# Image statistics dealt differently to half rounds, gather addresses cast in pairs, offset products issued behind the out-projection

## The chip, the cores and the metric

The kernel runs on one core of one Trainium2 chip. The metric is the device time of one execution in microseconds (us), the median of several runs. A profiled execution gives the trace from which every reading below is taken; it is one execution, with a time of its own.

## The reference

Eight images `x` of 512 channels and 64 x 64 pixels pass two layers, each of the form x = x + f(group_norm(x)).

```
x = x + deform_attention(_gn(x), w_q, w_off1, b_off1, w_off2, w_kv, w_out, b_out)
x = x + bottleneck(_gn(x), conv_w, ..., out_b)

# deform_attention, per image:
q     = w_q @ x                                   # 512 x 4096 pixels, 8 groups of 64 channels
t     = gelu(q[:, ::4, ::4] * w_off1 + b_off1)    # 16 x 16 sample places in each group
off   = tanh(w_off2 @ t) * 4                      # two offsets for each place and group
feats = bilinear sample of q at (grid + off)      # four neighbours each, weighted
k, v  = w_kv @ feats                              # 256 keys and values
out   = softmax((q * 0.125) . k) v                # 8 heads
y     = w_out @ out + b_out
```

The bottleneck is a 1x1 convolution to 32 channels, a strided depthwise convolution, two fully connected layers, a depthwise transposed convolution, and a 1x1 convolution back to 512 channels. `_gn` takes the mean and variance of groups of 16 channels over a whole image.

## The kernel before, in words

**Images and rounds.** An image is cut in 8 tiles of 512 pixels, a tile's attention in 4 head pairs. A *round* is one head pair of one tile; an image has 32 rounds, r = 0 to 31. In the main loop (the loop over `g` in the big function) a round issues, in this order: `weighted_values` (tile `pa`, L597), every second round `sum_exps` (`pn`, L624), `add_exps` on VectorE (`es`, L609), once in four rounds `invert` (the reciprocal L637 on VectorE and four small DMAs of SyncE), `logits` of the next round (`ps`, L579, with the exponential L587 on ScalarE), a `fill` of work beside it, `project_out` of the head pair of six rounds ago (`pp`, L666, taken out on VectorE by L673 and its statistics by L676), and a second `fill`. The list that a round leaves on TensorE is the same for all images, so the length of a round can be compared between images. Engines work their queues in order; the order of the code is the order of the queues.

**Half rounds.** The two fills make a round two half rounds. `phase[0]` is 0 in the first, ahead of the out-projection, and 1 in the second, behind it. `fill(200)` draws from the generator `next_image(b)` until that yields `None` (or 200 units are used): so a `yield None` ends a half round and a `yield 0` does not. `next_image` counts its half rounds in `slot`: slot 0 is the second half of round 5, odd slots are first halves, and slot 2(r-5) is the second half of round r. Out-projections, and with them the first fill, begin with round 6.

**What the fills carry.** Slots 0 to 26 work on the bottleneck of the image before (`layer1`, ending with `project_beside`, whose products are `po`, L892, in second halves from slot 12) and on the next image: its 8 tiles are loaded from slot 5, and from slot 12 the 32 `bn_stats` of `norm_x` (L201, VectorE) are drawn, 5 or 6 in each second half. A 33rd draw finds the generator at its end, and from the slot after that the four steps of `norm_q` and `group_stats` are drawn, one in each slot: `bn_aggr` (L169) in the first, then the small product `gps` (L173), then `gpsb` (L182), then the normalising of two tiles.

**The next image's queries.** In round 20 of images 1 to 6 `make_q` issues the whole query projection of the next image in one block (`pq`, L275; transposes `pqt`, L324; rows written to the DRAM tile `qd`). The last four transposes go to PSUM tiles that VectorE empties (L332). Behind it come two `tensor_reduce` of VectorE (L286). From then on `samples` holds that image's sampling generator.

**Sampling.** `sample` starts with the offset products (eight 128 x 128 by 128 x 4 products `po`, L424, each of two matmuls) and the tanh (L433, ScalarE), then `yield None`; then 17 short VectorE operations make the positions, weights and row numbers (L435 to L472), and L474 casts all 32 columns of row numbers to int32 (`row`). Then come 20 gather slots. In the first 16 GpSimd issues two gathers each (L518; four gathers fill one tile `g` of 128 x 4 x 2 x 64 numbers, of which there are two buffers); odd ones also hold `weigh` (L484 to L489, VectorE) of the tile whose last gather was issued a round before, and two of them `to_channels` (L494). Where `to_channels` ends, `project_k` and `project_v` follow in rounds 30 and 31.

**The start.** Image 0's sampling is interleaved with image 1's query projection by a loop that gives the projection 6 units of room for a `None` of `sample` and 2 for a 0. Image 1's sampling is begun there by one `next`, and goes on in image 0's rounds from the second half of round 5.

Of the kernel before, what the change touches and what calls it, by code (L numbers as in the profile page):

```python
# [25 lines left out]
HEADS = 8  # L26
# [23 lines left out]
def kernel(  # L50
# [15 lines left out]
    nc = tc.nc  # L66
# [29 lines left out]
    def spot(b, k):  # L96
        j = region[b]
        k %= NT + 1
        return spares[j] if k == 0 else regions[j][:, :, (k - 1) * TP : k * TP]
# [34 lines left out]
    def load_wq():  # L134
        nc.sync.dma_start(wbuf, w_qT.rearrange("(cc p) o -> p cc o", p=P))
# [13 lines left out]
    def col(k, n=1):  # L149
        return vec[:, k : k + n]  # L150
# [10 lines left out]
    def new_stats(which, b):  # L161
        return small.tile([P, NCC, NT, 6], F32, tag=f"st{which}", name=f"st{which}_{b}")
# [35 lines left out]
    def norm_x(b, st, order=range(NT)):  # L198
        for t in order:
            for cc in range(NCC):  # L200
                nc.vector.bn_stats(st[:, cc, t, :], x_tile(b, t)[:, cc, :])  # L201
                yield None
# [207 lines left out]
    def free_of(b):  # L410

        return spot(b, NT)

    def feats_of(b):
        return free_of(b)[:, 2:4, :].rearrange("p a (c k) -> p a c k", c=2)

    def sample(b, qd):

        free, feats = free_of(b), feats_of(b)
        po = ps_mm.tile([P, TP], F32, tag="mm", name=f"po_{b}")  # L420
        for h in range(2):
            for hp in range(NCC):
                k = h * 16 + hp * 4
                nc.tensor.matmul(  # L424
                    po[:, k : k + 4],
                    offset_in[b][h][:, hp * P : (hp + 1) * P],
                    col(V_OFF2, 4),
                    start=True,
                    stop=True,
                )  # L430

        pos = small.tile([P, 32], F32, tag="pos", name=f"pos_{b}")
        nc.scalar.activation(pos, po[:, :32], AF.Tanh)  # L433
        yield None
        nc.vector.scalar_tensor_tensor(  # L435
            pos, pos, OFF_SCALE, cst[:, K_BASE : K_BASE + 32], ALU.mult, ALU.add
        )
        nc.vector.tensor_scalar(pos, pos, 2.0 / 15.0, -1.0, ALU.mult, ALU.add)
        nc.vector.tensor_scalar(pos, pos, 1.0, float(HW), ALU.add, ALU.mult)
        nc.vector.tensor_scalar(pos, pos, -1.0, 0.5, ALU.add, ALU.mult)  # L440


        ci = small.tile([P, 32], I32, tag="ci", name=f"ci_{b}")
        nc.vector.tensor_copy(ci, pos)
        lo = small.tile([P, 32], F32, tag="lo", name=f"lo_{b}")
        wgt = small.tile([P, 2, 32], F32, tag="wgt", name=f"wgt_{b}")
        nc.vector.tensor_copy(lo, ci)
        nc.vector.tensor_tensor(wgt[:, 0, :], lo, pos, ALU.is_gt)
        nc.vector.tensor_sub(lo, lo, wgt[:, 0, :])
        yield 0  # L450
        nc.vector.tensor_scalar(lo, lo, 0.0, float(HW - 2), ALU.max, ALU.min)

        nc.vector.tensor_sub(wgt[:, 0, :], pos, lo)
        nc.vector.tensor_scalar_add(wgt[:, 1, :], wgt[:, 0, :], -1.0)
        nc.vector.scalar_tensor_tensor(wgt, wgt, -1.0, wgt, ALU.mult, ALU.max)
        nc.vector.tensor_scalar(wgt, wgt, -1.0, 1.0, ALU.mult, ALU.add)
        nc.vector.tensor_scalar_max(wgt, wgt, 0.0)
        yield 0
        lov = lo.rearrange("p (hg a) -> p hg a", a=2)
        wgtv = wgt.rearrange("p k (hg a) -> p k hg a", a=2)  # L460
        rowf = small.tile([P, 2, 16], F32, tag="rowf", name=f"rowf_{b}")
        wt = small.tile([P, 2, 16, 2], F32, tag="wt", name=f"wt_{b}")
        nc.vector.scalar_tensor_tensor(
            rowf[:, 0, :], cst[:, K_GRPNO : K_GRPNO + 16], float(N), lov[:, :, 0], ALU.mult, ALU.add
        )
        nc.vector.scalar_tensor_tensor(
            rowf[:, 0, :], lov[:, :, 1], float(HW), rowf[:, 0, :], ALU.mult, ALU.add
        )
        nc.vector.tensor_scalar_add(rowf[:, 1, :], rowf[:, 0, :], float(HW))
        for ky in range(2):  # L470
            for kx in range(2):
                nc.vector.tensor_mul(wt[:, ky, :, kx], wgtv[:, ky, :, 1], wgtv[:, kx, :, 0])  # L472
        row = small.tile([P, 2, 16], I32, tag="row", name=f"row_{b}")
        nc.vector.tensor_copy(row, rowf)  # L474

        held = []
        acc = [free[:, h, :].rearrange("p (g d) -> p g d", d=DH) for h in range(2)]

        def weigh(h, half, ky, g):

            i = h * HEADS + 4 * half
            w = wt[:, ky, i : i + 4, :].unsqueeze(3).to_broadcast([P, 4, 2, DH])
            a = acc[h][:, 4 * half : 4 * half + 4, :]
            nc.vector.tensor_mul(g, g, w)  # L484
            if ky == 0:
                nc.vector.tensor_add(a, g[:, :, 0, :], g[:, :, 1, :])
            else:
                nc.vector.tensor_add(a, a, g[:, :, 0, :])
                nc.vector.tensor_add(a, a, g[:, :, 1, :])  # L489

        def to_channels(h):
            pt = ps_mm.tile([P, TP], F32, tag="mm", name=f"pf_{b}_{h}")
            for cc in range(NCC):
                nc.tensor.transpose(  # L494
                    pt[:, cc * P : (cc + 1) * P],
                    acc[h][:, 2 * cc : 2 * cc + 2, :].rearrange("p g d -> p (g d)"),
                    ident,
                )
            nc.scalar.copy(
                feats[:, :, :, h * P : (h + 1) * P],  # L500
                pt.rearrange("p (a c k) -> p a c k", a=2, c=2),
            )

        steps = [(h, half, ky) for h in range(2) for half in range(2) for ky in range(2)]

        for slot in range(2 * len(steps) + 4):
            n, odd = divmod(slot, 2)
            if odd and n >= 5 and n % 4 == 1:
                to_channels(n // 4 - 1)
            if odd and 1 <= n <= len(steps):  # L510
                weigh(*steps[n - 1], held.pop(0))
            if n < len(steps):
                h, half, ky = steps[n]
                if not odd:
                    held.append(gp.tile([P, 4, 2, DH], F32, tag="g", name=f"g_{b}_{n}"))
                for i in (2 * odd, 2 * odd + 1):
                    k = h * HEADS + 4 * half + i
                    nc.gpsimd.indirect_dma_start(  # L518
                        held[-1][:, i, :, :].rearrange("p j d -> p (j d)"),
                        None,  # L520
                        qd[:, :],
                        bass.IndirectOffsetOnAxis(ap=row[:, ky, k : k + 1], axis=0),
                    )
            yield None
# [467 lines left out]
    phase = [1]  # L992
# [4 lines left out]
    def next_image(b):  # L997

        n = b + 1
        if b:  # L1000
            free = spot(b - 1, 0)
            first = layer1(b - 1, st1s.pop(b - 1), project_beside, free, free[:, 0:2, :])
            other, blocks = iter(()), ()
            if n < B:
                st = new_stats(0, n)
                blocks = norm_x(n, st)
                other = norm_q(n, st, norms)


            first_load = 5  # L1010
            ahead = 4
            slot = 0
            while first:
                if blocks is None and ahead:
                    next(other)
                    ahead -= 1
                if next(first, "end") == "end":
                    first = None
                if n < B:
                    if first_load <= slot < first_load + NT:  # L1020
                        load_x(n, (slot - first_load,), nc.gpsimd)
                    if slot == first_load + 2 * NT:
                        load_wq()
                    if phase[0] and slot > first_load + 6:
                        for _ in range(6 if slot in (first_load + 13, first_load + 15, first_load + 17) else 5):
                            if blocks and next(blocks, "end") == "end":
                                blocks = None
                slot += 1
                yield None
            if n < B:  # L1030
                drain(other)
                while n not in samples:
                    yield None
        if n < B:
            yield from samples[n]
# [6 lines left out]
    samples = {}  # L1042
# [15 lines left out]
    with tc.manual_schedule():  # L1058
# [38 lines left out]
        for g in range(len(names) + LAG):  # L1097
# [44 lines left out]
            k = g + 1 - LAG  # L1142
# [132 lines left out]
```

## Time and profile before

| | |
|---|---|
| runs (3) | 3301.49 us median, 3300.69 to 3302.63 |
| the profiled execution | 3300.22 us, of which the program's span 3298.4 us |
| TensorE matmul | 3212.1 us busy, 97% of the span |
| VectorE | 2321.9 us busy, 70% |
| ScalarE | 1187.9 us busy, 36% |
| GpSimd | 606.2 us busy, 18% |
| granted TensorE clock, mean | 0.99 |

A line of the timeline has a start and a duration in us, the engine, the line of the code, the operation, the tile it writes and those it reads, and, in brackets, how long the engine had been idle and what released it. In the view of waits a line names who waited, for whom, how long in total, how often, and the longest. A window's line gives busy time and count of each engine, the granted clock, and the DMA's share and GB/s. PE is TensorE, PEld its weight loads, DVE VectorE, ACT ScalarE, POOL GpSimd, SP SyncE.

### The profile page before, as it was taken

Reading aid. Unit: us, or ns where it says so; the run is one execution under the profiler, and the core shown is the slowest. Engines: PE = TensorE matmul, PEld = TensorE weight load, DVE = VectorE, ACT = ScalarE, POOL = GpSimd, SP = SyncE. Lnnn points to the kernel's source line nnn. Section 1 sums busy time; section 2 is a strip of 40 time slices with the busy share of each in tenths; the row PEclk is TensorE's granted clock in tenths of the full one; section 3 lists DMA queues with packets and bytes.
Section 4 is the critical chain, followed back from the end, with each engine's and each line's share of the span. In section 5 each row is a group of like instructions: output and inputs, shape, how many; then the busy total and the mean of one; then the engine's idle time right before and its main releaser. Section 6 shows DMA issues by size and latency. Waiting matters only on the chain.

```text
span 3298.4 us, 46059 instructions
## 1 busy us (share of the span) xinstructions
PE 3212.1 (97%) x18196; PEld 1532.3 (46%) x18196; DVE 2321.9 (70%) x3666; ACT 1187.9 (36%) x1641; POOL 606.2 (18%) x576
## 2 busy tenths in 40 slices
PE   6999999999999999999999999999999999999996
PEld 5884223258332583326732276332853338433222
DVE  7885765786757767587766876668766687756565
ACT  2343333344324433344333443335433344333420
POOL 1130300230402204022130312204021040310201
PEclk9999999999999999999999999999999999999996
DMA  7232222662327532284323833257232482322713
GB/s 275 77 99 73 81 69 87 202 134 78 116 77 224 122 90 91 96 224 113 111 85 132 197 91 105 79 188 171 71 97 89 179 179 65 122 71 71 135 38 131
DMA packets 293873, 390.61 MB, mean 118 GB/s; under 512 B 18320, under 2 KB 157840, under 8 KB 293648
## 3 DMA queue, kind: packets, MB, share of 16 engines
q1 hardware_dynamic: 240368, 261.72, 24.3%
q0 software_dynamic: 53280, 125.86, 17.3%
q8 instruction: 145, 2.38, 0.3%
q14 instruction: 80, 0.66, 0.1%
HBM read 193.52 MB, written 192.94 MB: 117 GB/s over the span
## 4 chain that ended last, share of the span: by engine, by line
PE 90%; DVE 6%; issue 2%; DMA 1%; SPq 0%; ACT 0%; POOL 0%; ACTq 0%; DVEq 0%; POOLq 0%
PE pp L666 25%; PE pq L275 24%; PE ps L579 13%; PE pa L597 12%; PE pqt L324 4%; PE pn L624 3%; PE py L749 2%; PE pk L532 2%; PE pv L559 2%; DVE rn L637 1%; PE po L892 1%; DVE st L201 1%; DMA rn<-rn 1%; DVE es L609 1%; DVE rb L650 1%
## 5 line engine op out<-in xcount | busy, mean ns | idle before, releaser
L666 PE MATMUL pp<-image,wout 128*64 128x512 f32 x3584 | 823.5, 602 | 4.9 <-DVE image L652 3.2
L587 ACT ACTIVATE es<-ps 128x1024 f32<-128x1024 f32 x512 | 505.3, 1023 | 289.3 <-PE ps L579 201.3
L666 PEld LDWEIGHTS pp<-image,wout 128*64 128x64 f32 x3584 | 238.0, 137 | 551.8 <-issue 465.5
L597 PE MATMUL pa<-es,vt 128*64 128x512 f32 x2048 | 488.3, 597 | 1.7 <-ACT es L587 1.7
L275 PE MATMUL pq<-image,wbuf 128*128 128x256 f32 x2048 | 476.2, 381 | 1.9 <-DVE image L217 1.9
L518 POOL DMA_INDIRECT g<-qd,row x256 | 274.2, 1071 | 1024.5 <-DVE row L474 842.1
L673 DVE SCALAR_TENSOR_TENSOR image<-pp,vec,image 128x512 f32<-128x512 f32 x224 | 166.8, 745 | 415.4 <-PE pp L666 383.1
L579 PE MATMUL ps<-image,kt 64*64 64x512 f32 x3584 | 442.6, 602 | 1.0
L275 PEld LDWEIGHTS pq<-image,wbuf 128*128 128x128 f32 x2048 | 381.8, 191 | 54.4 <-issue 5.0
L604 ACT COPY image<-pa 128x512 f32<-128x512 f32 x224 | 132.1, 590 | 683.7 <-PE pa L597 628.3
L609 DVE TENSOR_TENSOR es<-es,es 128x1024 f32<-128x1024 f32 x256 | 310.6, 1213 | 71.5 <-PE pa L597 71.4
L597 PEld LDWEIGHTS pa<-es,vt 128*64 128x64 f32 x2048 | 137.3, 136 | 298.0 <-issue 273.9
L579 PEld LDWEIGHTS ps<-image,kt 64*64 64x64 f32 x3584 | 115.5, 132 | 312.1 <-issue 184.6
L637 DVE RECIPROCAL rn<-pn 128x512 f32<-128x512 f32 x64 | 214.7, 3355 | 13.7 <-PE pn L624 6.9
L334 ACT COPY qr<-pqt 128x512 f32<-128x512 f32 x224 | 131.2, 586 | 237.2 <-PE pqt L324 222.2
L185 POOL TENSOR_TENSOR gs<-ve,nhalf 128x4 f32<-128x4 f32 x16 | 16.7, 1042 | 1063.3 <-DVE ve L184 1063.3
L650 DVE STREAM_SHUFFLE rb<-rn 128x512 f32<-128x512 f32 x256 | 187.4, 732 | 0.5 <-issue 0.4
L275 PE MATMUL pq<-es,es 128*128 128x256 f32 x768 | 181.5, 379 | 0.0
L944 POOL DMA_DIRECT2D out_dram<-part x126 | 138.0, 1324 | 161.0 <-ACT part L939 153.7
L201 DVE BATCH_NORM_STATS2 st<-image 128x6 f32<-128x512 f32 x256 | 158.6, 678 | 7.5 <-DMA image<-in_x_dram 7.4
L676 DVE BATCH_NORM_STATS2 st<-image 128x6 f32<-128x512 f32 x224 | 155.6, 695 | 7.7
L652 DVE TENSOR_TENSOR image<-image,rb 128x512 f32<-128x512 f32 x224 | 155.2, 693 | 7.8
(197 smaller groups left out, 3470.2 us busy)
## 6 DMA issues: line engine op xcount, KB each, us to landing
qd<-qr SPq DMA_DIRECT2D x256, 256.0 KB
image<-in_x_dram SPq DMA_DIRECT2D x112, 512.0 KB
out_dram<-image SPq DMA_DIRECT2D x49, 1024.0 KB
image<-in_x_dram POOLq DMA_DIRECT2D x48, 1024.0 KB
out_dram<-part POOLq DMA_DIRECT2D x126, 256.0 KB
image<-in_x_dram SPq DMA_DIRECT2D x16, 1024.0 KB
wbuf<-in_w_kvT_dram SPq DMA_DIRECT2D x14, 1024.0 KB
out_dram<-spare POOLq DMA_DIRECT2D x56, 256.0 KB
```

The lines of the kernel that those rows point to most:

```text
L201: nc.vector.bn_stats(st[:, cc, t, :], x_tile(b, t)[:, cc, :])
L275: nc.tensor.matmul(bank[:, o * 2 * P : (o + 1) * 2 * P], w[:, k, o * P : (o + 1) * P], xh[:, k, :], start=(k == 0), stop=(k == 1),)
L518: nc.gpsimd.indirect_dma_start(held[-1][:, i, :, :].rearrange("p j d -> p (j d)"), None, qd[:, :], bass.IndirectOffsetOnAxis(ap=row[:, ky, ...
L579: nc.tensor.matmul(ps[k : k + DH, a, :], kt[r : r + DH, hp, kc * P + k : kc * P + k + DH], qt[r : r + DH, hp, :], start=True, stop=True,)
L587: nc.scalar.activation(e, ps, AF.Exp)
L597: nc.tensor.matmul(pa[a * DH : (a + 1) * DH, :], vt[:, kc, hd * DH : (hd + 1) * DH], es[kc][:, a, :], start=(kc == 0), stop=(kc == 1),)
L609: nc.vector.tensor_add(es[0], es[0], es[1])
L637: nc.vector.reciprocal(rn, denominators.pop((b, t)))
L650: nc.vector.stream_shuffle(rb, rn, [2 * (hp % 2) + hp // 2] * 32)
L666: nc.tensor.matmul(pp[r : r + DH, :], wout[:, hp, oc * P + r : oc * P + r + DH], ao[:, hp, :], start=(hp == 0), stop=(hp == NCC - 1),)
L673: nc.vector.scalar_tensor_tensor(xt[:, oc, :], pp, col(V_BOUT + oc), xt[:, oc, :], ALU.add, ALU.add)
L676: nc.vector.bn_stats(st[:, oc, t, :], xt[:, oc, :])
```

## The change

Four edits. The tanh of `sample` is followed by `yield 0`, and `next_image` keeps waiting while `phase[0]` is 0: the offset products and the tanh are issued in the second half of round 20, behind the out-projection, in the half round that also holds the positions and the first two gathers. The single cast of all row numbers is replaced by a cast of two columns in each of the first 16 gather slots, ahead of its two gathers. And the statistics are drawn 5 in each second half, and 4 in slot 19, which is the first half of round 15.

```
@@ sample @@
         nc.scalar.activation(pos, po[:, :32], AF.Tanh)
-        yield None
+        yield 0
...
         row = small.tile([P, 2, 16], I32, tag="row", name=f"row_{b}")
-        nc.vector.tensor_copy(row, rowf)
...
                 if not odd:
                     held.append(gp.tile([P, 4, 2, DH], F32, tag="g", name=f"g_{b}_{n}"))
+                k = h * HEADS + 4 * half + 2 * odd
+                nc.vector.tensor_copy(row[:, ky, k : k + 2], rowf[:, ky, k : k + 2])
                 for i in (2 * odd, 2 * odd + 1):
@@ next_image @@
-                    if phase[0] and slot > first_load + 6:
-                        for _ in range(6 if slot in (first_load + 13, first_load + 15, first_load + 17) else 5):
+                    if slot == first_load + 14 or phase[0] and slot > first_load + 6:
+                        for _ in range(5 if phase[0] else 4):
                             if blocks and next(blocks, "end") == "end":
                                 blocks = None
...
                 drain(other)
-                while n not in samples:
+                while n not in samples or phase[0] == 0:
                     yield None
```

`first_load` is 5. Counted from the code, the 32 statistics go to the slots so:

| slot | 12 | 14 | 16 | 18 | 19 | 20 | 22 |
|---|---|---|---|---|---|---|---|
| before | 5 | 5 | 5 | 6 | 0 | 6 | 5 |
| after | 5 | 5 | 5 | 5 | 4 | 5 | 3 |

More of the change, by code (lines that the diff above doesn't have):

```diff
@@ L433, in sample @@
         nc.scalar.activation(pos, po[:, :32], AF.Tanh)
-        yield None
+        yield 0
         nc.vector.scalar_tensor_tensor(
@@ L473, in sample @@
         row = small.tile([P, 2, 16], I32, tag="row", name=f"row_{b}")
-        nc.vector.tensor_copy(row, rowf)
         held = []
@@ L515, in sample @@
                     held.append(gp.tile([P, 4, 2, DH], F32, tag="g", name=f"g_{b}_{n}"))
+                k = h * HEADS + 4 * half + 2 * odd
+                nc.vector.tensor_copy(row[:, ky, k : k + 2], rowf[:, ky, k : k + 2])
                 for i in (2 * odd, 2 * odd + 1):
@@ L1023, in next_image @@
                         load_wq()
-                    if phase[0] and slot > first_load + 6:
-                        for _ in range(6 if slot in (first_load + 13, first_load + 15, first_load + 17) else 5):
+                    if slot == first_load + 14 or phase[0] and slot > first_load + 6:
+                        for _ in range(5 if phase[0] else 4):
                             if blocks and next(blocks, "end") == "end":
@@ L1031, in next_image @@
                 drain(other)
-                while n not in samples:
+                while n not in samples or phase[0] == 0:
                     yield None
```

## The prediction

> **What bounds the kernel now.** I read the page's shares and chain, then TensorE's waits, then the length of every round (from one round's first `pa` to the next one's, in the timeline), then the rounds that are longer in some images than in others.
>
> ```profile
> PE 3212.1 (97%) x18196; PEld 1532.3 (46%) x18196; DVE 2321.9 (70%) x3666; ACT 1187.9 (36%) x1641; POOL 606.2 (18%) x576
> ...
> PE 90%; DVE 6%; issue 2%; DMA 1%; SPq 0%; ACT 0%; POOL 0%; ACTq 0%; DVEq 0%; POOLq 0%
> ```
>
> TensorE is the path: time can be won only where it waits or runs slowly. The view of its waits:
>
> ```profile
> PE gps L173 <- DVE mv L169: 39.7, 8, 29.7
> ...
> PE pp L666 <- ACT pos L433: 1.7, 6, 0.3
> ```
>
> 29.7 of the 39.7 us are one wait at the start; the same view over one image's stretch shows 1.2, once an image. Round lengths show more. Undisturbed rounds take 7.18 or 8.17 us. Round 20, which holds the query block, takes 122.64 us in four images and 124.34 in two (1 and 5). Round 24 takes 8.17 in images 1 to 3, 8.24 in 4, 11.42 in 5, 10.94 in 6.
>
> The wait for `mv`, in round 17 of image 4:
>
> ```profile
> 1886.00 1.21 DVE L609 TENSOR_TENSOR es<-es,es 128x1024 f32<-128x1024 f32 x1
> ...
> 1887.13 0.73 DVE L650 STREAM_SHUFFLE rb<-rn 128x512 f32<-128x512 f32 x1
> ...
> 1890.02 1.05 DVE L169 BATCH_NORM_AGGREGATE mv<-st 128x2 f32<-128x48 f32 x4
> ...
> 1891.22 0.35 PE L173 MATMUL gps<-mv,cst 128*128 128x4 f32 x2 [1.24 <-DVE mv L169]
> ```
>
> VectorE is without a gap from 1881.63 to here: it is late, and `gps` heads TensorE's queue.
>
> Round 20 of image 5, behind the query block:
>
> ```profile
> 2426.56 1.06 PE L424 MATMUL po<-vec,es 128*128 128x4 f32 x8
> ...
> 2428.55 0.20 ACT L433 ACTIVATE pos<-po 128x32 f32<-128x32 f32 x1 [1.34 <-PE po L424]
> ...
> 2428.80 5.35 PE L666 MATMUL pp<-image,wout 128*64 128x512 f32 x16 [0.29 <-ACT pos L433]
> ```
>
> The out-projection waits for the tanh and then takes 5.35 us in place of 3.65. A window there shows why; its last-but-two column, the granted clock, is 0.50:
>
> ```profile
> 2429.80:2433.20 3.40, 3.40 (x12) 0.96 (x10) 0.16 (x1) 0.00 (x0) 0.00 (x0) 0.50 0.98 319
> ```
>
> Round 24 of image 5:
>
> ```profile
> 2459.16 0.94 POOL L518 DMA_INDIRECT g<-qd,row  x1 [0.30 <-issue]
> ...
> 2459.32 5.20 PE L579 MATMUL ps<-image,kt 64*64 64x512 f32 x16
> 2460.41 0.95 POOL L518 DMA_INDIRECT g<-qd,row  x1 [0.30 <-issue]
> ...
> 2463.47 0.75 DVE L673 SCALAR_TENSOR_TENSOR image<-pp,vec,image 128x512 f32<-128x512 f32 x1 [8.75 <-remote]
> 2463.59 0.59 ACT L604 COPY image<-pa 128x512 f32<-128x512 f32 x1 [7.58 <-remote]
> ```
>
> `pp` had ended at 2456.7 and `pa` at 2458.4, but the engines that wait for them start 6.8 and 5.2 us late. From 2440.4 to 2461.4 GpSimd issues 17 gathers almost end to end; TensorE's signals come through when that run ends. Images 2 and 4 show the same lag in rounds 24 and 25, up to 3.5 us, without loss.
>
> [...] the 5.35 us count as busy. [...] dips of 3.413 us begin at 320.36, 828.95 and 2429.80, multiples of 3.413 apart. [...]
>
> **Part 1, statistics.** Counted from the code, slots 18, 19, 20, 22 take 5, 4, 5, 3 where they took 6, 0, 6, 5; both deals end in slot 22. A group of 5 takes 3.05 us, of 6 3.64, so 0.6 each. Round 17: slot 22 is shorter by 1.2 us, so `es` starts at 1884.8 (its `pa` ends at 1884.5). The shuffle needs the reciprocal's small DMAs: that reciprocal ended at 1881.67 and ends 0.6 earlier, since slot 20 has one statistic less. The quickest shuffles in the trace come 4.2 us behind theirs or less, so 1885.3; it starts behind `es`, at 1885.9, and `mv` is done at 1889.9. `pp` ends at 1890.0. The wait of 1.24 goes, and `pp` itself is next. The four in slot 19 take 2.45 us ahead of round 15's out of PSUM step, where VectorE has 2.24 us idle plus the 0.6 from slot 18; its data landed over 10 us before. If that cover is gone, up to 0.6 us a round, which TensorE does not wait for (two `pp` tiles). Six images: **-7.4 us** (bounds 0 and -7.4).
>
> **Part 2, offset products behind the out-projection.** All go along: 16 matmuls (1.95 us from 2426.56 to 2428.51) and the tanh; no DMA moves, and GpSimd's and SyncE's queues keep their order. `pp` needs only the PSUM copy that `po` needed, so starts at once: 0.29 x 6 = 1.7 us. Behind `po` comes `pa`, which waits for none of it. VectorE's positions now wait for the tanh some 0.7 us, but start 1.6 us earlier than before (image 3: 1632.3 against 1633.9), as the out-projection is taken out 2 us earlier. Queued behind that wait: `es` of round 21, still earlier than before. If `po` got the PSUM tile of `pp`, it would wait for L673, 0.9 us x 6. It should get the tile of the last transpose, freed earlier. **-1.7 us** (+3.7 to -1.7).
>
> The clock: the quiet stretch `po` + wait was 2.24 us; the two dips follow windows that hold it whole, in which other TensorE work fills 1.17 and 1.00 us of 3.41. Windows with 1.48 or 1.54 did not dip. After, the stretch is 1.95, leaving 1.46. I take both dips gone: 2 x 1.7 = **-3.4 us**. Bounds: 0, or two more dips, +3.4.
>
> **Part 3, casts.** One cast goes, 16 come, in 8 images: 120 more. The cast of 32 columns takes 0.17 us; that of two is not shown[...] 12 to 20 us of VectorE. In rounds 21 to 28 of image 3 VectorE is busy 50.1 us of 62.0, so 1.5 us free a round against 2 x 0.17. Hidden; with that cover gone, +20 us. GpSimd now waits for VectorE before each pair. A pair takes 0.3 + 0.95 + 0.3 + 0.95, landing 1.3 later: 3.8 us, and `weigh` comes a round (7.2) behind the cast. Gain: no run of 17; pairs with VectorE's work between them. I take the stalls of round 24 as gone: 3.2 + 2.8 + 0.1 = **-6.1 us** (bounds 0 and -6.1; the same lag at a new place could cost as much: +6).
>
> **The start.** Image 1's projection gets 4 units less room before the positions. TensorE waits little there, and all the work stays: 0, within 1 either way.
>
> **Sum**: 7.4 + 1.7 + 3.4 + 6.1 = 18.6 us from the profiled 3300.2 gives 3281.6. That execution is 1.27 us below the median 3301.49, so 3282.9: I say 3283.
>
> **Rivals.**
> The run of gathers is not the cause, or pairs still join: round 24 or a neighbour keeps its stall. For it: gathers of images 1 to 3 ran as densely and lost nothing. Against: every long lag in rounds 21 to 28 lies in such a run. 3283 + 6.1 = 3289. Chance 0.22.
> The statistics gain nothing, because the reciprocal's DMAs land late among the bottleneck's stores and the shuffle waits: 3283 + 7.4 = 3290. For: a landing under these stores is not timed. Chance 0.08.
> Nothing that can be told: `po` waits for L673 (+5.4), dips stay (+3.4) and round 24 stays (+6.1): 3298. Chance 0.08.
> Slower: each cast waits until the gathers that read the rest of `row` have landed. A pair lands 3.8 us after its cast, and the nearest next cast is some 2.2 us behind (the two steps of an out-projection, 0.75 + 0.69, and their wait): 1.6 us a round. From 1.1 on (1.5 free less two casts) it reaches TensorE: 0.5 x 8 rounds x 8 images = 32 us, or +13 net of 18.6: 3315. Against: POOL and DVE normalise different parts of one image at once (L217 at 1899.21 and 1902.73). Chance 0.07.
>
> **Numbers.** Likeliest case: 0.55. The range, 3278 to 3294, takes in the first two rivals, nearly both at once, and below a third dip gone (1.7, the one in image 0), the start (1) and some 2 us by which runs of one kernel differ (3300.69 to 3302.63). Measurement tells about 0.2%, 6.6 us, from no change. Faster 0.55 + 0.22 + 0.08 = 0.85, same 0.08, slower 0.07.
>
> **What would show it.** Right: no wait of `gps` for `mv` in rounds 17, no wait of `pp` for `pos`, round 20 at 122.3 us in six images, round 24 at 8.2, gathers in pairs. Wrong: rounds 21 to 28 above 7.2 or 8.2 us, casts with idle time before them, `po` waiting for L673, a long `ps`.

## The result and the profile after

The kernel after the change takes **3290.11 us** (median of 8 runs, 3287.14 to 3291.52). Beside it on the same chip the kernel before took 3300.27 us (8 runs, 3294.82 to 3302.63). The ratio is 0.9967 with a 95% interval of 0.9958 to 0.9976: 0.33% faster, 10.2 us. The forecast was 3283, a gain of 17 on these runs of the kernel before. The profiled execution took 3290.23 us, its span is 3288.5.

The page of the kernel after, the busy times and the chain:

```profile
PE 3207.7 (98%) x18196; PEld 1531.2 (47%) x18196; DVE 2330.8 (71%) x3786; ACT 1186.2 (36%) x1641; POOL 612.2 (19%) x576
...
PE 94%; DVE 4%; issue 1%; ACT 0%; DMA 0%; SPq 0%; POOL 0%; ACTq 0%; DVEq 0%; POOLq 0%
```

VectorE issues 120 instructions more and TensorE is still the path. The lengths of the rounds, from one first `pa` to the next one's, say where the time went (us; lines of the code have moved by one since):

| stretch | before | after | difference |
|---|---|---|---|
| span's start to first `pa` | 284.41 | 290.44 | +6.0 |
| round 17, images 1 to 6 | 9.98 each | 8.79 each | -7.1 |
| rounds 20 and 21, images 1 to 6 | 129.82, in two images 131.52 | 129.61, in one 129.85 | -4.4 |
| round 24, images 4, 5, 6 | 8.24, 11.42, 10.94 | 8.17 each | -6.1 |
| first `pa` to last `pa`, all | 2914.88 | 2897.28 | -17.6 |
| last `pa` to the span's end | 99.11 | 100.75 | +1.6 |

The three stretches in the middle did what was forecast (18.6 were forecast between the first `pa` and the last, 17.6 came). The start took 6.0 back and the end 1.6: -17.6 + 6.0 + 1.6 is -10.0, and the two spans differ by 9.9 (the rest is rounding).

**Round 17**, image 4, in the timeline of the kernel after:

```profile
1885.34 1.21 DVE L610 TENSOR_TENSOR es<-es,es 128x1024 f32<-128x1024 f32 x1
1886.47 0.73 DVE L651 STREAM_SHUFFLE rb<-rn 128x512 f32<-128x512 f32 x1
1886.86 3.65 PE L667 MATMUL pp<-image,wout 128*64 128x512 f32 x16
...
1889.35 1.05 DVE L169 BATCH_NORM_AGGREGATE mv<-st 128x2 f32<-128x48 f32 x4
...
1890.55 0.35 PE L173 MATMUL gps<-mv,cst 128*128 128x4 f32 x2
```

`gps` has no bracket any more: `mv` is done at 1890.40, `pp` at 1890.51. The view of TensorE's waits has 32.4 us for it where it had 39.7, and two waits in place of eight:

```profile
PE gps L173 <- DVE mv L169: 32.4, 2, 29.8
```

**Round 20**, image 5. The out-projection stands ahead of the offset products, ends at 2427.7, and nothing on TensorE waits for the tanh:

```profile
2424.05 3.65 PE L667 MATMUL pp<-image,wout 128*64 128x512 f32 x16
...
2429.51 1.94 PE L598 MATMUL pa<-es,vt 128*64 128x512 f32 x8
2429.62 0.20 ACT L433 ACTIVATE pos<-po 128x32 f32<-128x32 f32 x1 [4.93 <-PE po L424]
2429.85 0.19 DVE L435 SCALAR_TENSOR_TENSOR pos<-pos,cst 128x32 f32<-128x32 f32 x1 [0.62 <-ACT pos L433]
```

**Round 24**, image 5. The run of gathers is broken up, though into fours and not, as forecast, into pairs: the cast of the round's second pair is done at 2455.15, before the first pair's gathers end at 2457.09, so GpSimd goes on without a wait. It idles before each four only, here 1.44 us, until a cast of 0.16 us that stands behind other work of VectorE. `ps` takes 1.95 us where it took 5.20:

```profile
2453.54 0.16 DVE L516 CAST row<-rowf 128x2 int32<-128x2 f32 x1
2453.61 0.74 DVE L674 SCALAR_TENSOR_TENSOR image<-pp,vec,image 128x512 f32<-128x512 f32 x1
...
2453.97 0.94 POOL L519 DMA_INDIRECT g<-qd,row  x1 [1.44 <-DVE row L516]
...
2454.91 1.95 PE L580 MATMUL ps<-image,kt 64*64 64x512 f32 x16
2455.00 0.15 DVE L516 CAST row<-rowf 128x2 int32<-128x2 f32 x1
...
2455.21 1.88 POOL L519 DMA_INDIRECT g<-qd,row  x1 [0.30 <-issue]
...
2457.40 0.94 POOL L519 DMA_INDIRECT g<-qd,row  x1 [0.30 <-issue]
```

**The start.** TensorE alone, the instructions that waited between 155 us and the first `pa` (a wait of 0.47 us of `pk` for ScalarE, the same in both, is left out); first the kernel before:

```profile
263.32 2.06 PE L324 MATMUL pqt<-ident,image 128*128 128x128 f32 x15 [0.23 <-DVE image L391]
267.62 1.99 PE L532 MATMUL pk<-image,es 128*128 128x256 f32 x8 [0.29 <-ACT pos L433]
```

and the kernel after:

```profile
162.15 1.99 PE L275 MATMUL pq<-image,wbuf 128*128 128x256 f32 x8 [1.33 <-DVE spare L372]
221.84 1.99 PE L275 MATMUL pq<-image,wout 128*128 128x256 f32 x8 [1.07 <-DVE image L386]
265.21 1.99 PE L275 MATMUL pq<-image,wout 128*128 128x256 f32 x8 [0.77 <-ACT image L498]
267.99 2.06 PE L324 MATMUL pqt<-ident,image 128*128 128x128 f32 x15 [0.67 <-DVE image L391]
272.28 3.36 PE L533 MATMUL pk<-image,es 128*128 128x256 f32 x8 [0.29 <-ACT pos L433]
```

Three new waits and one longer, and `pk` takes 3.36 us in place of 1.99: a clock dip begins at 272.75. The work is the same, 704 matmuls. Over the stretch from 145 us to the first `pa` (columns: us, then TensorE's busy us and count), before and after:

```profile
145.00:284.40 139.41, 137.29 (x704) 117.64 (x705) 102.44 (x167) 49.96 (x81) 41.59 (x37) 1.00 0.35 101
```

```profile
145.00:290.44 145.44, 139.55 (x704) 118.39 (x705) 103.80 (x182) 49.68 (x81) 41.48 (x37) 0.99 0.34 96
```

TensorE idles 5.9 us where it idled 2.1 (+3.8), and is busy 2.3 longer, 1.4 of it in the dip.

### The profile page after: what moved, and what is told of

It reads as the page before. It is cut to its first block, busy times and chain, and to the rows that moved or that the text cites. A ratio compares the mean times of both kernels' runs of the same rounds, so it can differ in the third digit from the quotient of the medians.

```text
span 3288.5 us, 46198 instructions
## 1 busy us (share of the span) xinstructions
PE 3207.7 (98%) x18196; PEld 1531.2 (47%) x18196; DVE 2330.8 (71%) x3786; ACT 1186.2 (36%) x1641; POOL 612.2 (19%) x576
## 4 chain that ended last, share of the span: by engine, by line
PE 94%; DVE 4%; issue 1%; ACT 0%; DMA 0%; SPq 0%; POOL 0%; ACTq 0%; DVEq 0%; POOLq 0%
PE pp L667 27%; PE pq L275 23%; PE ps L580 14%; PE pa L598 13%; PE pn L625 4%; PE pqt L324 4%; PE pk L533 2%; PE py L750 2%; PE pv L560 2%; PE po L893 2%; DVE rn L638 1%; PE po L424 0%; PE pu L848 0%; DVE st L201 0%; PE po_s L893 0%
```

## Experiments

Each set of runs was made on one chip beside runs of the kernel before. That kernel took 3294.38, 3293.63, 3315.02 and 3316.01 us in the four sets, and 3300.27 at first, so the comparison inside a set comes first in what follows. The chip alone is not the reason: the first set and the fourth were made on a chip of the same number.

**1. The start put back**, in the kernel after:

```diff
-        for step in samples[0]:
-            room += 6 if step is None else 2
+        for i, step in enumerate(samples[0]):
+            room += 6 if step is None or i == 0 else 2
```

> The kernel after the change, with the first step of image 0's sample counted as 6 units of room at the start again (so image 1's projection stands where it stood before). Theory (the new order at the start costs 4.7 us of waits, and 1.4 us of a clock window): first pa back from 290.4 to about 284.4 us, time 3284 to 3285.5. Rival (the first pa is late because image 0's gathers now wait for their casts, in the start as elsewhere): first pa stays at 290, time 3290.

Measured: 3283.65 us (3282.09 to 3284.18) beside 3294.38, ratio 0.9966 (0.9954 to 0.9978), -10.7 us. First `pa` at 284.66. In the start the new waits are gone; the view of waits between 145 and 292 us, this kernel and then the kernel after:

```profile
PE pq L275 <- DVE image L386: 1.4, 1, 1.4
PE pqt L324 <- DVE image L391: 0.9, 2, 0.7
```

```profile
PE pq L275 <- DVE image L386: 2.5, 2, 1.4
PE pqt L324 <- DVE image L391: 1.3, 2, 0.7
PE pq L275 <- DVE spare L372: 1.3, 1, 1.3
PE pq L275 <- ACT image L498: 0.8, 1, 0.8
```

The casts are still in this kernel, so the rival (casts delay the start) falls. The order of the start is the term that was missed. This kernel is faster than both kernels: 10.7 us against the kernel before, where the kernel after gained 3.9 in a set with the same level of before (run 6).

**2. The start's new order alone**, in the kernel before:

```diff
-            room += 6 if step is None else 2
+            room += 6 if step is None and i else 2
```

(with `for i, step in enumerate(samples[0])` as above)

> The kernel before, with only the first step of image 0's sample counted as 2 units instead of 6 at the start. Theory of the order: first pa at 289 to 290.5 us, time 3305 to 3306.5, all else as before. Rival (image 0's casts delay the start): first pa at 284.4, time 3300.3, no change.

Measured: 3298.78 us (21 runs) beside 3294.38, ratio 1.0015 (1.0008 to 1.0021), +4.4 us; first `pa` at 289.44, without a clock dip in the start. So the order costs 4.4 us by the times and 3.8 to 5.0 by the first `pa` (the kernel before has it at 284.41 and, in run 5, at 285.69), less than the 6.0 seen first, which held a dip of 1.4. One thing was not expected at all: this kernel has the gathers of the kernel before, and its round 24 takes 8.17 us in every image.

**3. All 16 casts ahead**, in the kernel after: the same VectorE work, but no pacing.

```diff
         row = small.tile([P, 2, 16], I32, tag="row", name=f"row_{b}")
+        for ky in range(2):
+            for k in range(0, 16, 2):
+                nc.vector.tensor_copy(row[:, ky, k : k + 2], rowf[:, ky, k : k + 2])
...
-                k = h * HEADS + 4 * half + 2 * odd
-                nc.vector.tensor_copy(row[:, ky, k : k + 2], rowf[:, ky, k : k + 2])
```

> The kernel after, with all 16 casts of two columns issued together where the single cast of 32 columns stood, so that VectorE does the same work and the gathers are no longer paced. Theory (runs of gathers hold up TensorE's signals, the pacing is what removed the stalls): runs of 8 to 17 gathers end to end come back, and rounds 24 or 25 take 10 to 12 us in some images; 3294 to 3297, that is +4 to +7 on the kernel after. Rival (any earlier start of the gathers, or the new order, removed the stalls): round 24 stays at 8.17, time 3290, within 1.5.

Measured: 3290.94 us beside 3294.38, ratio 0.9990 (0.9984 to 0.9997). The runs of 16 gathers are back, and round 24 takes 8.17 us in every image. Image 5, round 22 to 24:

```profile
2452.67 0.94 POOL L520 DMA_INDIRECT g<-qd,row  x1 [0.30 <-issue]
2453.45 0.75 DVE L675 SCALAR_TENSOR_TENSOR image<-pp,vec,image 128x512 f32<-128x512 f32 x1 [2.82 <-PE pp L668]
2453.92 0.94 POOL L520 DMA_INDIRECT g<-qd,row  x1 [0.30 <-issue]
2455.16 0.59 ACT L606 COPY image<-pa 128x512 f32<-128x512 f32 x1 [4.20 <-PE pa L599]
```

GpSimd issues end to end, yet VectorE and ScalarE are released by TensorE, and in time; in the kernel before the brackets said "remote". My theory, that a run of gathers holds up TensorE's signals wherever it comes, fell here: a run alone is not enough.

**4. The casts in pairs alone**, in the kernel before (one cast out, the cast of two columns in each even and odd slot in, as in the change).

> The kernel before, with only the casts in pairs. Theory (pacing alone removes the stalls of round 24): round 24 takes 8.2 us in every image, all else as before, time 3294 (-6.1). Rival (the stalls hang on the order of the offset products, which starts the gathers at another time): stalls stay, time 3300, or above it by what the casts cost VectorE.

Measured: 3294.04 us beside 3294.38, ratio 0.9999 (0.9990 to 1.0007). Nothing gained and nothing lost. By the level of the kernel before, and by run 2's profile, there was no stall to remove in this set. The gathers come mostly in fours here too.

**5. The kernel before again**, profiled.

> The kernel before, unchanged, profiled beside the others, since the kernel with only the new order at the start (before's runs of 16 gathers) showed no stall in round 24, and the kernel before took 3294.4 us there. Theory (whether TensorE's signals come late depends on the chip or the session, and runs of gathers alone don't do it): either round 24 takes 8.17 us in all images and the time is about 3294, or stalls are there and it is about 3300. Rival (runs of gathers always do it, and the two experiments escaped by their start): stalls of 2.8 to 3.3 us in round 24 of two images, 3300.

Measured: 3294.22 us beside 3293.63, ratio 1.0003. Round 24 takes 8.17 us in all images, though image 5's first 16 gathers are issued as densely as in the first profile. So the 6.1 us of stalls in the first profile belonged to the set of runs as well as to the kernel.

**6. The kernel after again**, in the set of run 5.

> The kernel after, unchanged, on the chip of these runs. Theory: 3289 to 3290.5 in either case, so that against before it gains 10 where before has stalls in round 24, and only 4 to 5 us where it has none (7.1 statistics, 1.3 order, 1.7 a clock dip, less 6 at the start). Rival (the change gains 10 us wherever it runs): 3284 where before takes 3294.

Measured: 3289.75 us (3287.80 to 3290.48) beside 3293.63, ratio 0.9987 (0.9979 to 0.9996): 3.9 us, not 10. The two profiles (5 and 6) differ by 5.5 us: +4.5 before the first `pa`, -9.6 from there to the last, -0.4 behind it.

**7. All casts ahead again**, in the same set.

> The kernel after with all 16 casts issued together ahead, so runs of 16 gathers come back; once more, beside before and after. If before shows stalls of round 24 here: theory (the runs are needed for them) 10 to 12 us in round 24 of some image, 3294 to 3297; rival 8.17 and 3290. If before shows none: both 3290 to 3291.

Measured: 3290.38 us, ratio 0.9992 (0.9983 to 1.0000), 0.6 above run 6; runs of 16 gathers, no stall.

**8. The statistics alone**, in the kernel before:

```diff
-                    if phase[0] and slot > first_load + 6:
-                        for _ in range(6 if slot in (first_load + 13, first_load + 15, first_load + 17) else 5):
+                    if slot == first_load + 14 or phase[0] and slot > first_load + 6:
+                        for _ in range(5 if phase[0] else 4):
```

> The kernel before with only the statistics dealt anew. Theory: round 17 takes 8.79 in place of 9.98 us in six images, gps waits no more for mv there, all else as before: -7.1 on before. Rival (VectorE's work in slot 19 delays something else, or the clock takes some back): -2 to -5.

Measured: 3290.33 us (21 runs, 3286.04 to 3292.63) beside 3293.63, ratio 0.9989 (0.9982 to 0.9996): -3.3 us, though round 17 takes 8.79 us in all six images, which is -7.1. The profile shows where some of it went. Windows at 828, 1627 and 2426 us (the column of 0.50 is the granted clock): round 20 of images 1, 3 and 5 has a dip.

```profile
828.39:831.80 3.41, 3.31 (x8) 1.00 (x10) 1.25 (x2) 0.04 (x1) 0.00 (x0) 0.50 0.98 252
1627.11:1630.52 3.41, 3.41 (x8) 0.96 (x10) 1.12 (x1) 0.00 (x0) 0.00 (x0) 0.50 0.97 289
2425.82:2429.23 3.41, 3.41 (x10) 0.95 (x12) 1.08 (x1) 0.00 (x0) 0.00 (x0) 0.50 1.00 292
```

In both kernels' first profiles and in this one the dips of an execution lie whole multiples of 3.413 us apart: 149 and 618 of them from the dip at 320.36 us of the kernel before to those at 828.95 and 2429.80, 16 from that at 272.75 of the kernel after to its next, and 234 each time between the three dips here. From the program's start they do not lie alike: the first dip of the kernel before lies at 320.36 us in the first profile and at 322.92 in run 5's, 2.56 apart, and a dip at 828.95 in the first profile and at 828.39 here, 0.56 apart. I call the stretches of 3.413 us that are counted from an execution's dips its windows, and estimate from these figures how the length of an image fits them. Undisturbed, it is 399.66 us with the old deal of the statistics (117.09 windows) and 398.48 with the new (116.74); a dip adds 1.7 us, half a window. In this kernel an image with a dip and the next one without make 400.17 + 398.48 us, 234.0 windows, so the offset products meet the same point of a window in every second image: the three dips lie 798.7 us apart. With the old deal, by the same estimate, the place moves by 0.59 of a window over an image with a dip and by 0.09 over each one without; the two profiles that have two dips have them four images apart. Five profiles of the old order and the old deal have 2, 1, 2, 1 and 1 dips in rounds 20, this one has 3. The five have 1.4 on average, so some 1.6 dips more, of 1.7 us each, would give back 2.7 of the 7.1. That this kernel has 3 in most executions rests on one profile, and 1 us is not accounted for.

**9. The offset products' new place alone**, in the kernel before, with the start as it was:

```diff
         nc.scalar.activation(pos, po[:, :32], AF.Tanh)
-        yield None
+        yield 0
...
-                while n not in samples:
+                while n not in samples or phase[0] == 0:
```

> The kernel before with only the offset products put behind the out-projection (the first step of image 0's sample counted as 6 units, so the start is as before). Theory (pp needn't wait for the tanh, and the quiet stretch is short enough for the clock): rounds 20 and 21 together 0.2 us shorter in six images, no clock dip in round 20, where the five profiles with the old order show 9 dips (1.8 each, 1.7 us apiece): -1.3 - 3.1 = -4.4 on before. Rival (the clock dips just move to other places): -1.3 or less.

Measured: 3290.74 us beside 3315.02, ratio 0.9929 (0.9916 to 0.9941). Rounds 20 and 21 are 0.2 us shorter and no round 20 has a dip, as the theory said; nor has one in the seven other profiles with the new place. What was not foreseen is the size, 24.3 us, in a set in which the kernel before was 21 us slower than in the sets above. One cast still serves all gathers here, but the run is broken up all the same. GpSimd's waits, image 5:

```profile
POOL g L518 <- DVE row L474: 125.2, 1, 125.2
POOL g L518 <- issue: 6.1, 20, 0.3
POOL g L518 <- DVE image L486: 3.3, 2, 1.8
```

The gathers start earlier in their rounds, and the ninth needs a buffer `g` that `weigh` has not yet read: GpSimd waits 1.8 us for it, so eight and eight gathers in place of 16. In image 0 a run of 12 is left, and there the profile has a lag: ScalarE copies `pa` out at 336.62, 2.1 us after it ended, without loss to TensorE. Eights do not rule a lag out either: in the first profile image 2's gathers come eight and eight, and its round 25 has the copy at 1268.74, 3.5 us after the end of `pa`.

**10. Statistics and new place without the paced casts**: the kernel after with the start put back (as in 1) and one cast of 32 columns.

> The kernel after with the start restored and the single cast of 32 columns in place of the 16, so runs of up to 16 gathers come back: parts 1 and 2 of the change alone. Theory, where before takes about 3294 us and shows no stall in round 24: 3283 to 3284.5, as with the paced casts, that is the casts gain nothing there. Where before takes about 3300: stalls of round 24, 3287 to 3290, against 3284 with paced casts. Rival (pacing gains everywhere): 3287 to 3290 also where before takes 3294.

Measured: 3284.06 us (3282.24 to 3289.50) beside 3315.02, ratio 0.9908 (0.9894 to 0.9922). That is the time of run 1 within 0.4 us, without the casts, also where the kernel before stalls. The profiled execution is the longest of the five, 3289.5 us, and shows one stall, in round 6 of image 0, whose gathers still come 12 in a run:

```profile
334.51 0.94 POOL L518 DMA_INDIRECT g<-qd,row  x1 [0.30 <-issue]
336.10 1.02 ACT L587 ACTIVATE es<-ps 128x1024 f32<-128x1024 f32 x1 [4.63 <-PE pa L597]
337.65 0.75 DVE L673 SCALAR_TENSOR_TENSOR image<-pp,vec,image 128x512 f32<-128x512 f32 x1 [8.19 <-remote]
```

The run's last gather ends at 335.45; ScalarE is released 0.65 us behind it and VectorE 2.2, where it was 2.1 to 2.2 us for both in the first profile.

**11. The casts alone once more** (the kernel of run 4).

> The kernel before with only the casts in pairs, again, since whether before stalls differs from chip to chip. Where before takes 3299 us or more (stalls): theory (pairs with VectorE's cast between them break up the runs, which suffices) no round 24 above 8.3, 3293 to 3296; rival (only the earlier gathers of the new order, which wait for a buffer after eight, remove them) 3299 or more. Where before takes about 3294 both say 3294, and nothing new is learnt.

Measured: 3294.07 us (3293.45 to 3294.93) beside 3316.01, ratio 0.9934 (0.9920 to 0.9947): -21.9 us, and no round 24 above 8.2. The paced casts alone suffice too. With run 9: by the times, each of the two edits by itself takes away what the kernel before loses in such a set, and the second adds nothing to that.

**12. More room at the start**, in the kernel after:

```diff
-            room += 6 if step is None else 2
+            room += 12 if i == 0 else 6 if step is None else 2
```

(with `for i, step in enumerate(samples[0])` as in 1)

> The kernel after, with the first step of image 0's sample counted as 12 units of room at the start (6 in the kernel with the start restored, 2 in the kernel after). Theory (what counts is only which product of image 1's projection stands beside which step of image 0's sample, and 6 is where TensorE waits least): first pa between 284.5 and 287 us, 3284 to 3287, no better than with 6. Rival (the more of image 1's projection goes ahead of the sample, the less TensorE waits): first pa at 282 to 284, 3280 to 3283.

Measured: 3286.24 us (3285.65 to 3287.77) beside 3316.01, ratio 0.9910 (0.9895 to 0.9925); first `pa` at 286.87, with a clock dip at 269.59. Both are within what was expected, and behind run 1: more room is no better. That the places of single steps count is the reading that fits; it was not taken further.

## Why the prediction was right and where it was wrong

**Right in direction, 7 us too hopeful in size.** The failed step is the prediction's "The start": "TensorE waits little there, and all the work stays: 0, within 1 either way". It measured +6.0 in the first pair of profiles; undone, the kernel takes 3283.65 us, and done alone it costs 4.4. All the work does stay; the error is to read the few waits of the old order as a property of the stretch. They belong to the order. Two things stand in it that a look at the program would have shown. VectorE's operations for the positions (L435 to L449, 1.7 us) come ahead of L372 with less room, and a product of image 1 waits for L372, 1.33 us. And the transposes and copies of image 0's features (L493, L498) move by some products, so that two of these wait for L386 and for ScalarE's copy, 1.07 and 0.77 us. The dip at 272.75, 1.4 us, is not the order's own: with the old order of the start two of eight profiles have one there too (at 269.38 in run 4, 268.60 in run 8), and runs 2 and 3, with the new one, have none.

**Part 1: right.** 1.19 us a round, forecast 1.24; six images, -7.1 for -7.4. `mv` was forecast to end just ahead of `pp`, and ends 0.1 us ahead. The rival in which the reciprocal's DMAs hold up the shuffle fell: it starts behind `es`, without a gap. Alone, the edit shows only 3.3 us in the median (run 8), in part, by the estimate there, since its profile has 3 dips in rounds 20 where five others have 1.4 on average.

**Part 2: right.** Waits for the tanh: forecast -1.7, measured -1.3. The two dips went (-3.4), and none came elsewhere in the images. The reason given for them holds in all fourteen profiles. In the six with the products in their old place, a dip follows every window of 3.413 us (counted from the dips of the same profile) of round 20 in which TensorE work other than `po` fills at most 1.28 us of the 3.41, and none in which it fills 1.40 or more; in the eight with the new place the least is 1.60, and no round 20 has a dip. (Two readings of the prediction are off: by the timeline both of its windows hold about 1.18 us, the 1.00 leaving out 0.17 us of `pqt` ahead of `po`, and the least of the windows without a dip in those rounds is 1.77, not 1.48.) With the start put back, the change gives 10.7 us in a set where the kernel before does not stall: 7.1 + 1.3 + about 1.4 dips of 1.7 is 10.8. Apart, part 1 gave 3.3 there; part 2 was run alone only where the kernel before stalls, so its share there is not measured.

**Part 3: right in its number, half right in its reason.** Round 24 lost its stalls, -6.1 as forecast. The gathers came in fours where pairs were forecast, so the rival "pairs still join" was right on that, but the fours brought no stall. The casts are hidden: 128 of 0.158 us, 20.2 in all, and run 4 finds them at no cost (the low end of the forecast's 12 to 20 us was the author's estimate). The rival "each cast waits for earlier gathers" fell with the first profile (idle before the casts: 0.0 us in all). But pacing was not needed for it in this kernel, since part 2 already breaks up the runs (runs 9 and 10), and how much there is to gain is set by something outside the kernel: nothing in the sets at 3294, 6.1 us in the first profile, about 22 in the sets at 3315 and 3316. The -6.1 is measured against one profile of the kernel before; run 5's profile of the same kernel has none of it. That the kernel before still took near 3300 us beside the kernel after was luck.

That the 21 us of the sets at 3315 and 3316 are such stalls is inferred: two ways of breaking up the run remove them, and run 10 caught one, but the kernel before was not profiled in such a set. Two rivals are untested. In those sets no other kernel with runs of 16 was run (the statistics alone would be one), so it is not shown that an edit which leaves the runs whole would not have done as much. And the kernel before had a mean granted clock of 0.987 to 0.990 in them, against 0.990 to 0.992 in the sets at 3294; as an estimate from these figures, the clock was some 0.002 lower on average, which over 3315 us is about 7 of the 21 us, as a consequence of stalls or apart from them. What makes TensorE's signals come late during a run of gathers in one set and not in another stays open. Whether they do also sets what the change is worth: 3.9 us in a set at 3294 (run 6), 10.2 in the first.

**The end.** +1.6 us had no step of the prediction. The code there is the same, and the two executions of the kernel before took 99.1 and 101.1 us for it, run 8 took 97.9, the kernel after 100.8 and 100.7, each with two to four stretches at a granted clock of 0.50. So the 1.6 us lie within what executions differ by, and are not the change; whether the places of these stretches make the difference is not shown.

The number 3290 is also about what two rivals gave, 3289 and 3290, and neither occurred: a time near a rival's does not show that rival, only its place in the profile does.

## What to carry to other kernels

When steps of two interleaved pieces of work are moved against each other, list which operation then stands ahead of which on every queue, at each place where they meet; a stretch without waits in the old order says nothing on the new one (here the new order cost 3.8 to 5.0 us by the first `pa`). Before a stall is made the target of an edit, see it in more than one set of runs, and find out whether a neighbouring edit removes it already. Parts that touch a clock dip need not add up (part 1 took 7.1 us of waits away and gave 3.3 alone): take them together and apart.

## What the hardware showed that was not expected

The same program took 3293.6 to 3316.0 us, by the set of runs. In the two slowest sets the four other kernels that were run, all with the run of 16 indirect gathers broken into eights or fours, took 3284 to 3294 us. Under a run, consumers of TensorE were released up to 6.8 us late in the first profile, up to 4.6 us late in run 10's, and not late at all in the profiles of runs 2, 3, 5 and 7, with gathers of the same pace (1.25 us each).

A cast of two columns took 0.158 us and one of 32 columns 0.173: here the number of casts counted, hardly their width.

TensorE did not stand still ahead of the clock dips of round 20 (first profile: busy 3.1 us of the 3.41 ahead of each). There, with the offset products in their old place (six profiles), a dip followed the windows of 3.41 us with up to 1.28 us of other matmuls beside these products, which are four columns wide, and none with 1.40 us or more.

An image of 398.48 us in place of 399.66 came with 3 dips in rounds 20 (run 8, one profile) where five profiles had 1 or 2. By estimate from the dips' distances, the offset products then met the same place in a window of 3.413 us in every second image.
